# First lot's radial network among the senders' features, all statistics in front, edge indices and three tiles' gram products behind

## The chip, the cores and the metric

The kernel runs on one core of one Trainium2 chip. The metric is the device time of one execution in microseconds (us). Engines: PE is TensorE (matmul), PEld its weight load, DVE is VectorE, ACT is ScalarE, POOL is GpSimd, SP is SyncE; DMAs are issued by SP, ACT and POOL. A "q" behind an engine's name (SPq, ACTq) means its instruction queue, where DMA issues stand.

## The reference, cut to what matters

A network of two layers over 1250 nodes with 512 features. Each layer adds a graph part and a linear attention to the layer-normed features, then a layer of experts. The change lies in the first graph part, which has 41250 edges:

```python
xn = _layernorm(x, axis=-1)
x0, x1 = _lin_irreps(x0, x1, W_up0, W_up1)          # of xn: the senders' features
h = edge_feats                                       # 8 per edge
for W in (W_mlp1, W_mlp2, W_mlp3):                   # the radial network
    h = SILU_2MOM * jax.nn.silu(h @ W / jnp.sqrt(jnp.float32(W.shape[0])))
tpw = h @ W_mlp4 / jnp.sqrt(jnp.float32(W_mlp4.shape[0]))
w1, w2, w3, w4 = jnp.split(tpw, 4, axis=-1)
s0 = x0[sender]
s1 = x1[sender]
# p1 to p4: products of w1 to w4, s0, s1 and four edge attributes
msg0 = jax.ops.segment_sum(m0, receiver, num_segments=num_nodes)
msg1 = jax.ops.segment_sum(m1, receiver, num_segments=num_nodes)
```

The attention of this layer has no softmax, so the kernel needs of the nodes only the gram matrix xn^T xn (512 x 512).

## The kernel before

**Nodes.** The nodes stand in ten tiles of 125 rows. `PIECES` groups tiles 0, 1 to 2, 3 to 5 and 6 to 9, as they are loaded. For a piece, `piece` computes the statistics of its tiles (BN_STATS and BN_AGGR on DVE, one Sqrt on ACT, one reciprocal on DVE), and then `sender(t)` for each tile: DVE makes the normed features xn (L296, L297); PE transposes them (ptr, L302); DVE copies the result to xT (L303); PE multiplies it with the up-weights (pu, L306); ACT scales it to us (L309) and issues two DMAs that write it to xup in DRAM; PE adds the tile's share to the gram matrix in four products (L312), whose accumulators pga, pgb and pgf stay in PSUM for all ten tiles.

**Edge indices.** After the third piece, an `issue_after` block holds the index work: w4b's last quarter is scaled (L331), the receivers (dg) are cast and reduced to a smallest and a largest receiver for each group of seven edge tiles, PE brings these to all partitions (pg, L343), and DVE derives base, rel, idx, the source's quarter (shi, slo) and code from them (L345 to L389, `window`).

**The edge loop.** 323 edge tiles of 128 edges go through `edges`, two at a time; 16 tiles are a lot, with one run of the radial network for it. `layer(b, l, h)` is layer l of lot b: PE into two "net" banks of PSUM, then two Silus on ACT (half of h each, from a buffer of four). For a tile, `product` gathers the senders' rows from xup (POOL, sg, L443) and multiplies h with w4b (pw, L448); `messages` forms msg on DVE (L454 and L457); `gather` multiplies msg with masks sy into pd (L591 to L597); every seven tiles pd is added to agg in DRAM by an indirect DMA (L602). The masks of a group come from `factors` (oh, sy; DVE and ACT, L428 to L436). Six sg buffers let POOL run ahead. Layers of the next lot are issued at tiles 0, 4 and 8 of a lot, the edge features (ef) of the lot after that at tile 6; at tile 10 of each lot but the first, one of `steps` is issued (loads, then the attention's small products). Lot 0's network stands in front of the loop, behind the last piece (L416 to L419), and then four copies of the gram matrix to gs (L420).

**Order and queues.** The tile framework's scheduler places each instruction on its engine's queue, in the program's order as far as its own costs and the `issue_after` marks allow. An engine's queue is strictly in order. SP issues the loads, the clearing of agg (13 DMAs, 6.6 MB) behind the edge features of lots 0 and 1, later loads for the steps, and the clearing of adj behind the edge features of lot 3. The eight semaphores of the hardware DMA queues are shared by SP's and ACT's DMAs, one outstanding DMA each: an issue waits until the DMA before it on its semaphore has landed, whichever engine issued that one. PSUM has two "mm" banks (pga and pgb, later pd), two "net" banks (pu, pg, ph) and four "in" banks (pgf; ptr, later pw).

Of the kernel before, what the change touches and what calls it, by code (L numbers as in the profile page):

```python
# [10 lines left out]
F32 = mybir.dt.float32  # L11
# [3 lines left out]
AF = mybir.ActivationFunctionType  # L15
OP = mybir.AluOpType
# [6 lines left out]
P = 128  # L23
R = 125
NT = N // R
# [4 lines left out]
EG = -(-ET // GT)  # L30
BT = 2 * GT
HID = 64
# [24 lines left out]
def tile_graph_layers(ctx: ExitStack, tc: tile.TileContext, i: dict, out: bass.AP):  # L57
# [17 lines left out]
    def ps_tile(tag, name):  # L75
        return ps_[0].tile([P, 512], F32, tag=tag, bufs=ps_[1][tag], name=name)
# [131 lines left out]
    with ExitStack() as s0:  # L208
# [82 lines left out]
        def sender(t):  # L291


            xn = ew.tile([P, D], F32, tag="xn", bufs=3, name="xn")
            q = dict(scalar1=mvs[:R, t, 0:1], scalar2=rss[:R, t:t + 1], op0=OP.subtract, op1=OP.mult)
            V.tensor_scalar(xn[:R, :P], X[:R, t, :P], **q)  # L296
            last[0] = V.tensor_scalar(xn[:R, P:].rearrange("p (m u) -> p m u", m=3),  # L297
                                      X[:R, t, P:].rearrange("p (u m) -> p m u", m=3), **q)
            ps = in_tile("ptr")
            v = ps[:, :4 * R].rearrange("p (k r) -> p k r", k=4)  # L300
            for k in range(4):
                T.transpose(v[:, k, :], xn[:R, k * P:(k + 1) * P], ident[:R, :R])  # L302
            V.tensor_copy(xT[:, :, t * R:(t + 1) * R], v)  # L303
            pu = ps_tile("net", "pu")
            for k in range(4):
                T.matmul(pu[:R, k * P:(k + 1) * P], xT[:, k, t * R:(t + 1) * R], wu[:, min(k, 1), :],  # L306
                         start=True, stop=True)
            us = ew.tile([P, D], F32, tag="us", bufs=4, name="us")
            S.mul(us[:R], pu[:R], 1.0 / math.sqrt(P))  # L309
            spread(nc.scalar, xup.rearrange("(p t) d -> p t d", t=NT)[:, t, :], us[:R])  # L310
            for pg, a, b, k in gram:
                T.matmul(pg[:, a:b], xn[:R, k * P:(k + 1) * P], xn[:R, k * P:], start=t == 0 and a == 0,  # L312
                         stop=t == NT - 1, skip_group_check=True)

        last = [None]

        def piece(a, b):
            with tc.issue_after(last[0].ins) if last[0] else ExitStack():
                for t in range(a, b):
                    st = ew.tile([P, V.BN_STATS_DIM], F32, tag="bst", bufs=3, name="n0s")  # L320
                    V.bn_stats(st[:R], X[:R, t, :])
                    V.bn_aggr(mvs[:R, t, :], st[:R])
                S.activation(rss[:R, a:b], mvs[:R, a:b, 1], AF.Sqrt, bias=eps[:R], scale=1.0)
                V.reciprocal(rss[:R, a:b], rss[:R, a:b])
            for t in range(a, b):
                sender(t)

        for a, b in PIECES[:3]:
            piece(a, b)
        with tc.issue_after(last[0].ins):  # L330
            V.tensor_scalar(w4b[:, 3 * P:], w4b[:, 3 * P:], 1.0 / math.sqrt(3.0), None, op0=OP.mult)  # L331

            dgf = ew.tile([NG, GW * P], F32, tag="h", bufs=4, name="dgf")
            V.tensor_copy(dgf, dg)
            ext = ec.tile([NG, 2], F32, name="ext")
            V.tensor_reduce(ext[:, 0:1], dgf, AX.X, OP.min)
            V.tensor_reduce(ext[:, 1:2], dgf, AX.X, OP.max)
            V.tensor_tensor(ext[:, 1:2], ext[:, 1:2], ext[:, 0:1], op=OP.subtract)
            extb = ec.tile([NG, 2, P], F32, name="extb")
            V.tensor_copy(extb, ext[:, :, None].to_broadcast([NG, 2, P]))  # L340
            pg0 = ps_tile("net", "pg0")
            for a in range(2):
                T.matmul(pg0[:, a * NG:(a + 1) * NG], extb[:, a, :], ident[:NG, :NG], start=True, stop=True)  # L343
            base = ec.tile([P, 2, NG], F32, name="base")
            V.tensor_copy(base, pg0[:, :2 * NG].rearrange("p (a g) -> p a g", a=2))  # L345
            npf = ec.tile([P, 1], F32, name="npf")
            V.tensor_reduce(npf, base[:, 1, :], AX.X, OP.max)
            npi = ec.tile([P, 2], I32, name="npi")
            V.tensor_copy(npi[:, 0:1], npf)
            V.tensor_scalar(npi[:, 1:2], npi[:, 0:1], 5, None, op0=OP.arith_shift_right)  # L350
            V.tensor_scalar(npi[:, 0:1], npi[:, 1:2], 1, None, op0=OP.add)


            pc = ec.tile([P, 3], I32, name="pc")
            G.iota(pc[:, 0:1], pattern=[[0, 1]], base=0, channel_multiplier=1)
            V.tensor_scalar(pc[:, 1:2], pc[:, 0:1], 5, None, op0=OP.arith_shift_right)
            V.tensor_scalar(pc[:, 2:3], pc[:, 0:1], W - 1, None, op0=OP.bitwise_and)
            pcf = ec.tile([P, 3], F32, name="pcf")
            V.tensor_copy(pcf, pc)
            rows = ec.tile([P, 1], F32, name="rows")  # L360
            V.scalar_tensor_tensor(rows, pcf[:, 1:2], float(NPAD), pcf[:, 2:3], op0=OP.mult, op1=OP.add)


            EP = NG * GW
            rel = ec.tile([P, EP], F32, name="rel")
            V.memset(rel, 0.0)
            V.tensor_copy(rel[:, :ET], dstc)
            rel3 = rel.rearrange("p (g j) -> p g j", j=GW)
            V.tensor_tensor(rel3, rel3, base[:, 0, :, None].to_broadcast([P, NG, GW]), op=OP.subtract)
            srcf = ec.tile([P, ET], F32, name="srcf")  # L370
            V.tensor_copy(srcf, srcc)
            shi = ec.tile([P, ET], F32, name="shi")
            V.tensor_scalar(shi, srcf, float(LO), None, op0=OP.is_ge)
            for c in (2, 3):
                V.scalar_tensor_tensor(shi, srcf, float(c * LO), shi, op0=OP.is_ge, op1=OP.add)
            V.scalar_tensor_tensor(slo[:, 0, :], shi, -float(LO), srcf, op0=OP.mult, op1=OP.add)
            V.scalar_tensor_tensor(slo[:, 1, :], shi, float(LO), srcf, op0=OP.mult, op1=OP.subtract)
            bs = ec.tile([P, NG], F32, name="bs")
            cd = ec.tile([P, 2, ET], F32, name="cd")

            def window(code, idx):

                V.tensor_scalar(bs, base[:, 0, :], float(N), rows, op0=OP.min, op1=OP.add)
                V.tensor_copy(idx, bs)
                V.tensor_scalar(cd[:, 0, :], rel[:, :ET], 0.0, None, op0=OP.is_ge)
                V.scalar_tensor_tensor(cd[:, 0, :], rel[:, :ET], float(W), cd[:, 0, :], op0=OP.is_lt, op1=OP.mult)
                V.scalar_tensor_tensor(cd[:, 1, :], shi, float(W), rel[:, :ET], op0=OP.mult, op1=OP.add)
                V.scalar_tensor_tensor(cd[:, 1, :], cd[:, 1, :], 1.0, cd[:, 0, :], op0=OP.add, op1=OP.mult)
                V.tensor_scalar(code[:, :ET], cd[:, 1, :], -1.0, None, op0=OP.add)  # L389

            def layer(b, l, h):

                two = range(min(2, EG - 2 * b))
                ps = [ps_tile("net", "ph") for _ in (two if l != 1 else range(2))]
                half = [slice(0, HID), slice(HID, P)]
                if l == 0:
                    for q in two:
                        r = slice(32 * q, 32 * q + 16)  # L400
                        T.matmul(ps[q], w1b[r], h[r].rearrange("k j e -> k (j e)"), start=True, stop=True)
                else:
                    w = (w2b, w3b)[l - 1]
                    for q in two:
                        for p in range(2):

                            a, c = (q, p) if l == 1 else (p, q)
                            T.matmul(ps[c][half[a]], w[half[c]], h[half[c], a, :], start=True, stop=True)  # L408
                o = ew.tile([P, 2, 512], F32, tag="h", bufs=4, name="h")
                for n, x in enumerate(ps):  # L410
                    r = slice(0, HID * len(two)) if l == 1 else slice(0, P)
                    S.activation(o[r, n, :], x[r], AF.Silu, scale=1.0 / math.sqrt(8.0) if l == 0 else SILU_2MOM / 8.0)  # L412
                return o
            window(code0, idx0)
        piece(*PIECES[3])
        first = efs[0][0]  # L416
        with tc.issue_after(last[0].ins):
            for l in range(3):
                first = layer(0, l, first)  # L419
        for pg, a, b, k in gram:  # L420
            S.copy(gs[:, k, k * P:], pg[:, a:b])

# [1174 lines left out]
```

## Time and profile before

| | us |
|---|---|
| median of 3 runs (lowest to highest) | 2175.81 (2175.56 to 2176.47) |
| the profiled execution's own time | 2173.73 |
| its span, first to last instruction | 2171.9 |
| first sender product (pu) on PE | 13.6 |
| last write of xup issued | 54.5 |
| first gather of senders' rows (sg) | 58.2 |
| first message (L454) | 67.4 |
| first product of messages (pd) | 69.0 |
| last message of the edge loop | 588.7 |
| mean granted clock of TensorE | 0.973 |

The profile is of one execution; its times are us from its first instruction. A line of the timeline has the start, the duration, engine, source line, operation, output and inputs, the number of instructions merged, and in brackets the idle time before and what ended it. A line of the table by stages has the stretch, its length and then the busy time of each engine with the number of its instructions.

### The profile page before, as it was taken

Reading aid. Unit: us, or ns where it says so; the run is one execution under the profiler, and the core shown is the slowest. Engines: PE = TensorE matmul, PEld = TensorE weight load, DVE = VectorE, ACT = ScalarE, POOL = GpSimd, SP = SyncE. Lnnn points to the kernel's source line nnn. Section 1 sums busy time; section 2 is a strip of 40 time slices with the busy share of each in tenths; the row PEclk is TensorE's granted clock in tenths of the full one; section 3 lists DMA queues with packets and bytes.
Section 4 is the critical chain, followed back from the end, with each engine's and each line's share of the span. In section 5 each row is a group of like instructions: output and inputs, shape, how many; then the busy total and the mean of one; then the engine's idle time right before and its main releaser. Section 6 shows DMA issues by size and latency. Waiting matters only on the chain. (4 is left out here: it accounts for less than half of the span.)

```text
span 2171.9 us, 29920 instructions
## 1 busy us (share of the span) xinstructions
PE 2039.8 (94%) x11341; PEld 1109.4 (51%) x11341; DVE 891.1 (41%) x1864; ACT 640.7 (29%) x1665; POOL 635.3 (29%) x589
## 2 busy tenths in 40 slices
PE   7899999989886899999998999978999999999999
PEld 5334444434364646565566666644446655444354
DVE  7688888868757323232233300004000124670000
ACT  3443444434222424243343311115112121241000
POOL 1677777787600323222322211102000020002000
PEclk9899999989997899999999999989999999999999
DMA  8977777757653875958376312413001040200000
GB/s 257 309 203 179 203 200 189 191 137 189 156 146 104 268 225 153 280 145 239 70 235 165 71 25 64 141 31 111 1 0 64 15 95 0 65 7 1 14 14 19
DMA packets 132866, 270.60 MB, mean 125 GB/s; under 512 B 22028, under 2 KB 45396, under 8 KB 132569
## 3 DMA queue, kind: packets, MB, share of 16 engines
q0 software_dynamic: 48048, 124.53, 24.3%
q1 hardware_dynamic: 82952, 140.78, 20.3%
q10 hardware_dynamic: 1694, 3.07, 0.5%
q8 instruction: 99, 1.62, 0.3%
q14 instruction: 73, 0.60, 0.1%
HBM read 248.73 MB, written 44.76 MB: 135 GB/s over the span
## 5 line engine op out<-in xcount | busy, mean ns | idle before, releaser
L443 POOL DMA_INDIRECT sg<-xup,srcc x323 | 311.7, 965 | 165.9 <-issue 63.0
L457 DVE TENSOR_TENSOR msg<-pw,sg 128x768 f32<-128x768 f32 x323 | 305.4, 946 | 0.0
L971 PE MATMUL phd<-hu,ew 128*128 128x256 f32 x1280 | 292.9, 385 | 10.3 <-ACT hd L972 8.0
L979 PE MATMUL pye<-ew,hd 128*128 128x512 f32 x640 | 287.3, 593 | 0.0
L971 PEld LDWEIGHTS phd<-hu,ew 128*128 128x128 f32 x1280 | 243.8, 193 | 50.1 <-ACT hd L972 14.6
L591 PE MATMUL pd<-msg,sy 128*32 128x320 f32 x646 | 215.9, 448 | 29.3 <-DVE msg L457 28.5
L593 PE MATMUL pd<-msg,sy 128*32 128x256 f32 x1938 | 197.8, 394 | 0.0
L448 PE MATMUL pw<-w4b,h 64*128 64x512 f32 x646 | 187.0, 655 | 0.0
L979 PEld LDWEIGHTS pye<-ew,hd 128*128 128x128 f32 x640 | 117.5, 190 | 124.3 <-issue 122.8
L454 DVE TENSOR_TENSOR msg<-pw,sg 128x256 f32<-128x256 f32 x323 | 134.5, 416 | 78.0 <-PE pw L448 38.8
L436 ACT ACTIVATE sy<-oh,y 128x32 f32<-128x32 f32 x646 | 145.9, 312 | 6.1 <-DVE oh L428 3.3
L204 POOL DMA_INDIRECT adj<-sa,idx x47 | 81.6, 1736 | 220.4 <-ACT sa L203 122.9
L200 DVE TENSOR_SCALAR los<-iol,slo 128x314 f16<-128x314 f16 x230 | 58.2, 304 | 199.4 <-PE pa L201 199.4
L591 PEld LDWEIGHTS pd<-msg,sy 128*32 128x32 f32 x646 | 54.4, 109 | 161.5 <-DVE msg L457 93.6
L972 ACT ACTIVATE hd<-phd,b 128x256 f32<-128x256 f32 x160 | 75.8, 474 | 174.5 <-PE phd L971 174.5
L1414 PE MATMUL pyf<-w,hd 128*125 128x512 f32 (+1 forms) x280 | 125.1, 599 | 0.0
L991 POOL DMA_INDIRECT xrow<-yo,slot x23 | 36.3, 1577 | 298.6 <-ACT yo L990 284.9
L1400 PE MATMUL ph<-uT,w 128*128 128x500 f32 (+3 forms) x336 | 120.8, 515 | 1.1 <-ACT hd L1402 1.0
L989 DVE TENSOR_TENSOR yo<-pye,b 128x512 f32<-128x512 f32 x20 | 13.8, 690 | 244.4 <-PE pye L979 231.3
L597 PEld LDWEIGHTS pd<-msg,sy 128*32 128x32 f32 x1938 | 80.7, 112 | 56.0 <-issue 4.0
L412 ACT ACTIVATE h<-ph 128x512 f32<-128x512 f32 (+1 forms) x124 | 68.2, 591 | 135.5 <-PE ph L408 93.7
L597 PE MATMUL pd<-msg,sy 128*32 128x64 f32 x1938 | 94.1, 221 | 0.0
(424 smaller groups left out, 2650.1 us busy)
## 6 DMA issues: line engine op xcount, KB each, us to landing
ew<-in_L_ffn_W SPq DMA_DIRECT2D x104, 1024.0 KB
agg<-zero SPq DMA_DIRECT2D x12, 512.0 KB
adj<-zero SPq DMA_DIRECT2D x12, 512.0 KB
ag<-agg SPq DMA_DIRECT2D x10, 560.0 KB
ad<-adj POOLq DMA_DIRECT2D x10, 547.8 KB
sg<-xup,srcc POOLq DMA_INDIRECT x323
g<-in_L_gnn_W SPq DMA_DIRECT2D x4, 1024.0 KB
w<-in_L_ffn_W SPq DMA_DIRECT2D x4, 852.5 KB
```

The costliest lines, as they stand in the source:

```text
L436: S.mul(sy[:, j, c, :], oh[:, j, :], y4[:, t0 + j, c:c + 1])
L443: G.indirect_dma_start(out=sg, out_offset=None, in_=xup[:, :], in_offset=bass.IndirectOffsetOnAxis(ap=srcc[:, t:t + 1], axis=0))
L448: T.matmul(pw, h[hb:hb + HID, q, (j // 2) * P:(j // 2 + 1) * P], w4b[hb:hb + HID, :], start=True, stop=True)
L454: V.tensor_tensor(msg[:, :, 0, :], w_[:, 0], sg[:, None, :P].to_broadcast([P, 2, P]), op=OP.mult)
L457: V.tensor_tensor(msg[:, :, 1:, :], w_[:, 1, :, None, :].to_broadcast(q), s1[:, None].to_broadcast(q), op=OP.mult)
L591: T.matmul(d[:W, :SW], sy[:, j, 0, :], mf.rearrange("p a u -> p (a u)")[:, :SW], **q)
L593: T.matmul(d[c * W:(c + 1) * W, :2 * P], sy[:, j, c, :], mf[:, 4:5 + c:c, :], start=j == 0, stop=False, skip_group_check=True)
L597: T.matmul(d[c * W:(c + 1) * W, 2 * P:SW], sy[:, j, 0, :], mf.rearrange("p a u -> p (a u)")[:, a:a + 64], start=False, stop=q["stop"], ski ...
L971: mm = T.matmul(ph[:, :UT], ew1[q][:, k, f * P:(f + 1) * P], hu[:, k, :], start=k == 0, stop=k == 3)
L979: mm = T.matmul(py, hd[q][:, f, a * P:(a + 1) * P], ew2[q][:, f, :], start=q == 0 and f == 0, stop=q == 3 and f == 3)
L1400: mm = T.matmul(ph[:m, :c], w1[k][:, f * P:f * P + m], uT[:, k, c0:c1], start=k == 0, stop=k == 3)
L1414: T.matmul(py[:R], hd[f][:m, r0:r0 + R], w2[f // 4][:m, f % 4, :], start=f == 0, stop=f == FT - 1)
```

## The change

`piece` is split into `stats` (the statistics) and the loop over the tiles. The statistics of the last piece are now issued with those of the third, in front of tiles 3 to 5. `sender` returns its gram products as a function; they are called at once for tiles 0 to 6, and for tiles 7 to 9 after all senders. `layer` is moved up unchanged, and lot 0's three layers, with the scaling of w4b, are issued after tile 5. The index work now stands behind all senders and their gram products.

```diff
             spread(nc.scalar, xup.rearrange("(p t) d -> p t d", t=NT)[:, t, :], us[:R])
-            for pg, a, b, k in gram:
-                T.matmul(pg[:, a:b], xn[:R, k * P:(k + 1) * P], xn[:R, k * P:], start=t == 0 and a == 0,
-                         stop=t == NT - 1, skip_group_check=True)
+
+            def grams():
+                for pg, a, b, k in gram:
+                    T.matmul(pg[:, a:b], xn[:R, k * P:(k + 1) * P], xn[:R, k * P:], start=t == 0 and a == 0,
+                             stop=t == NT - 1, skip_group_check=True)
+            return grams
 
         last = [None]
 
-        def piece(a, b):
+        def stats(a, b):
             with tc.issue_after(last[0].ins) if last[0] else ExitStack():
                 for t in range(a, b):
...
                 V.reciprocal(rss[:R, a:b], rss[:R, a:b])
+
+        def layer(b, l, h):
...
+            return o
+        later = []
+        for n, (a, b) in enumerate(PIECES):
+            if n < 3:
+                stats(a, b)
+            if n == 2:
+                stats(*PIECES[3])
             for t in range(a, b):
-                sender(t)
-
-        for a, b in PIECES[:3]:
-            piece(a, b)
+                later.append(sender(t))
+
+                if t < NT - 3:
+                    later.pop()()
+                if t == 5:
+                    first = efs[0][0]
+                    with tc.issue_after(last[0].ins):
+                        V.tensor_scalar(w4b[:, 3 * P:], w4b[:, 3 * P:], 1.0 / math.sqrt(3.0), None, op0=OP.mult)
+                        for l in range(3):
+                            first = layer(0, l, first)
+        for x in later:
+            x()
         with tc.issue_after(last[0].ins):
-            V.tensor_scalar(w4b[:, 3 * P:], w4b[:, 3 * P:], 1.0 / math.sqrt(3.0), None, op0=OP.mult)
 
             dgf = ew.tile([NG, GW * P], F32, tag="h", bufs=4, name="dgf")
...
-            def layer(b, l, h):
...
             window(code0, idx0)
-        piece(*PIECES[3])
-        first = efs[0][0]
-        with tc.issue_after(last[0].ins):
-            for l in range(3):
-                first = layer(0, l, first)
         for pg, a, b, k in gram:
             S.copy(gs[:, k, k * P:], pg[:, a:b])
```

The order of instructions on each engine, before and after, differs only in the first part of the program, up to the first two lots of the edge loop. There, PE has lot 0's layer 0 behind tile 5, its layers 1 and 2 among tile 6's products, then the transposes of tiles 7 to 9, one gram product, the three tiles' pu, the other gram products, pg, layer 0 of lot 1 and the first pw. DVE has the casts and reductions of dg in front of the xT copies of tiles 7 to 9, and the four sums ssum (L500) among the index work; of the masks, two groups stand in front of the first messages, where there were three with the oh of three more. On SP, the edge features of lots 2 and 3 stand in front of most loads for the steps, and the clearing of adj behind those loads.

## Prediction

> **What bounds the kernel now.** The page says that PE works 94% of the span, and its chain of waits only reaches the last expert layer, so what the change is worth must be read at the start.
>
> ```profile
> span 2171.9 us, 29920 instructions
> PE 2039.8 (94%) x11341; PEld 1109.4 (51%) x11341; DVE 891.1 (41%) x1864; ACT 640.7 (29%) x1665; POOL 635.3 (29%) x589
> ```
>
> Next, the busy time by stages (columns: PE, PEld, DVE, ACT, POOL, then granted clock, DMA share, GB/s):
>
> ```profile
> 32.00:36.40 4.40, 0.92 (x6) 0.52 (x4) 4.40 (x20) 1.29 (x6) 0.00 (x0) 1.00 1.03 389
> 36.40:42.00 5.60, 4.99 (x19) 3.45 (x20) 5.60 (x13) 3.76 (x18) 0.00 (x0) 0.70 1.01 376
> 42.00:53.30 11.30, 11.30 (x63) 7.67 (x61) 6.09 (x9) 6.90 (x24) 0.00 (x0) 1.00 0.88 289
> 53.30:65.30 12.00, 8.32 (x27) 2.28 (x26) 4.70 (x7) 6.60 (x15) 5.54 (x6) 0.68 0.89 242
> 65.30:73.40 8.10, 8.10 (x53) 2.88 (x54) 4.87 (x8) 1.60 (x4) 3.84 (x5) 0.63 0.66 229
> 73.40:95.00 21.60, 17.53 (x231) 7.84 (x232) 16.37 (x28) 8.95 (x35) 14.59 (x15) 1.00 1.03 398
> 95.00:120.00 25.00, 23.32 (x294) 10.19 (x291) 23.46 (x41) 9.98 (x37) 17.92 (x18) 1.00 0.82 227
> 120.00:300.00 180.00, 173.97 (x2003) 78.38 (x1998) 154.75 (x268) 77.15 (x285) 134.73 (x128) 0.99 0.74 193
> ```
>
> The edge loop runs at PE's pace once it is under way (97% from 120 to 300 us); before it PE waits twice, at 33 to 36 and from 53 to 65, and pays with a low clock each time. The timeline names the waits:
>
> ```profile
> 32.27 0.64 PE L343 MATMUL pg<-ident,extb 47*128 47x47 f32 x4
> 36.41 0.33 PE L302 MATMUL ptr<-ident,xn 125*128 125x125 f32 x1 [3.50 <-DVE xn L296]
> 58.24 1.06 POOL L443 DMA_INDIRECT sg<-xup,srcc  x1 [50.12 <-DMA w<-in_L_mix_Wk]
> 65.28 3.79 PE L448 MATMUL pw<-w4b,h 64*128 64x512 f32 x8
> 67.39 0.42 DVE L454 TENSOR_TENSOR msg<-pw,sg 128x256 f32<-128x256 f32 x1 [8.08 <-PE pw L448]
> ```
>
> Tile 6's features wait for DVE's index work. Later the radial network, a chain PE to ACT to PE from 53.33, holds the first pw until 65.28 and the first message until 67.39, while the gathers have been coming since 58.24. The loop then meets the clearing of adj:
>
> ```profile
> 81.60:95.10 13.50, 5.87 (x7) 1.00 1.03 393
> 95.10:118.10 23.00, 15.12 (x16) 1.00 0.81 236
> DMA packets 2762, 9.43 MB, mean 377 GB/s; under 512 B 374, under 2 KB 502, under 8 KB 2761
> q1 hardware_dynamic: 1666, 6.11, 61.7%
> q0 software_dynamic: 1095, 3.31, 37.6%
> ```
>
> The first two lines are the long half of the messages (L457): 1.93 us a tile at a DMA share of 1.03, then 1.44 us. The others are all transfers of 70 to 95 us: SP's clears take 0.244 MB/us of 0.377.
>
> **The change, part by part.** No instruction is added or dropped, and from about 130 us on every engine's order is the old one; the sum is how much earlier the loop runs.
>
> *All statistics in front.* Four BN_STATS at 0.60 us start to start, four aggregations and a reciprocal, some 2.9 us, move ahead of tile 3's features. DVE waited 0.28 and 1.95 us for grams there, so most is covered: following DVE's order, tile 3's xT copy ends about 0.8 us later, and PE with it. Without that cover 2.9. Tile 5's grams end at 32.3 + 0.8 = 33.1.
>
> *The index work leaves.* PE no longer waits 3.50 us before tile 6, and 36.4 to 42 is not run at 0.70.
>
> *The network comes in.* Layer 0 costs PE 1.13 (row at 53.33) and is done at 34.2; tile 6's transposes and two grams fill PE until 36.4. ACT copies tile 5 (0.60), issues two xup writes (0.31 and up to 1.26, as at 32.70), loads its table (1.28) and runs Silu, 0.55 a half: the first half is there at 36.7. Layer 1 (1.09) ends at 37.8, the rest of tile 6's grams at 38.6, layer 2 at 39.9; tile 6's pu waits for a "net" bank and ends at 41.1. Behind ACT's Silus waits tile 6's copy, whose write goes out near 41.8, as before (42.32). What leaves is the chain of 12 us at 53.3.
>
> *Tiles 7 to 9.* Transposes 3 x 0.59, one gram 0.9, three pu at 1.1: 47.1. The xT copies stand behind index casts and two reductions on DVE: tile 9's features need tile 6's grams (38.6), 0.95 + 3.3 us of index work, and three copies at 0.6: 44.8, in time. The last xup write is issued at 49.2 to 50.5 instead of 54.51; write to first gather took 3.4 us (54.82 to 58.24), so the gathers start at about 53.3, 5 us earlier. Their flight no row shows alone; it lies between nothing and the 9.2 us from 58.24 to the first message. I take 4, in the lower half, since less else is in flight there than at 81.60 to 95.10: 57.3. On SP the edge features of lots 2 and 3 move ahead of lnb and Wk; lot 3's wait for lot 1's layer 0 (about 55), and the loads of wo, Wk, bk and bl and the clears of adj queue behind them until about 60 to 64.
>
> *Grams and indices behind.* The grams left, 1.4 + 2.3 + 2.3 (a tile's four rows at 28 to 32 us), end at 53.1, pg at 53.6. DVE has meanwhile done the source indices and ssum (4 x 1.39) by 52.7, so base waits for PE. Then, start to start from the rows of 32.95 to 36.51: base to the second cd 2.2, sb 0.4, oh 0.28, cd, sy, code and oh 1.5: the first message half begins at 58.0 instead of 67.39. One sy stands between its halves: L457 at 58.9 instead of 67.73. ACT's fourteen sy (3.08) run from 56.5 to 59.6. First pd at 59.9 instead of 68.99: **9 us earlier**.
>
> *Given back in lots 0 and 1.* DVE gets four oh, one sy, kvb and bqb, 2.5 us that lay in idle time. Where DVE sets the pace (95 to 120: 23.46 of 25) that costs up to 2.5, where gathers do, nothing; I take 0.5, since gathers do until 95. Those loads, 1.8 MB, ran in front of the loop and now fall into it. At 0.244 MB/us that is 7.4 us more of SP traffic, which also starts some 8 us earlier (62 instead of 70), so it ends near 95 again. Tiles by then: five at 62, then 33 / 1.93 = 17, so tile 22 where now it is tile 16, of which I count 5.5 ahead: 5.5 x 1.44 = 7.9, less 0.5, gives **7.5**. Bounds: 3.6 if the 1.8 MB cost the gathers their full time at 377 GB/s (4.8) and DVE its 0.5 on top of a 9 us gain, and 12 if the old clock of 0.63 (8.1 us, so 3.0 lost) goes as well and nothing is given back.
>
> The Trainium skill speaks against this part ("DMA: Bandwidth & Descriptors", Rules for kernel authors): transfers issued from different engines run on the same 16 DMA engines and interleave. By that rule the earlier gathers only share what is there and the sum would be nearer 2172; the row of 81.60 to 95.10 agrees that they share.
>
> Span 2171.9 - 7.5 = 2164.4; the profiled execution had 1.83 around its span, so 2166.2; the median of the runs lies 2.08 above that execution: **2168.3**.
>
> **Rivals.** *The transfers take it:* the loop starts 9 us earlier, but gathers, loads and clears move the same bytes at 377 GB/s, so only some 3.6 us are kept: 2172.2. For: share 1.03 and three DVE waits on sg between 80 and 95. Against: by the DMA shares over time the engines are half idle at 47 to 49 and 68 to 72 us, and the change fills these gaps.
>
> *More than forecast:* PE keeps its clock and the clears don't slow the first lots: 11 us, 2164.8. Against: the waits on sg.
>
> *A cold PE at the start of the loop:* after the first pw PE stands about 2.2 us before the first pd. If base comes 1.3 us later than I have it, this becomes the 3.5 us after which the clock was 0.70 for 5.6 us: 1.7 + 1.3 lost, 2171.3. The Trainium skill ("TensorE: Matmul & The Clock Gate", the HAM clock gate) puts the limit at one idle window of about 3.4 us; the 3.50 us row agrees.
>
> *Slower:* tiles 7 to 9's xup writes share semaphores with clears of agg, and each waits until an earlier one landed. In the old run tile 5's second issue took 1.26 us amid the clears. If the clears still fill the queue at 46 to 50, the writes queue behind one another, each up to 5.9 us (SP's own longest wait on such a write); three in a row put the gathers at 64 instead of 53.3 and, with 4 us of flight, messages at 68, and the loads inside the loop then cost 4.8: 2181. It decides from gathers later than 58 on. Against: 12 x 0.5 MB at 380 GB/s from 28 us are through by 47.
>
> **How the numbers follow.** Forecast 0.61, transfers 0.17, more 0.08, cold PE 0.06, slower 0.08. About 0.2% (4.35 us) is what a measurement of this kernel can tell from no change; that is below 2171.5 and above 2180.2. Of the forecast nine tenths lie below 2171.5, and all of "more", half of "cold" and a quarter of "transfers": 0.55 + 0.08 + 0.03 + 0.04, about 0.70. Slower 0.07; the rest 0.23. The range leaves out the end of "more" (0.07) and "slower" with the tail of "transfers" (0.12): 2163.0 to 2174.5.
>
> **What would show it.** Right: no 3.5 us idle of PE before tile 6's transposes; first gather near 53, first L454 near 58 with base released by pg, first pd near 60; L457 of tile 16 near 86 and of tile 22 near 95; the loop's last message 7 to 8 us before 588.7; later stages of equal length. Wrong: gathers after 58, a PE clock under 0.8 at the start of the loop, or the lead of 9 us at tile 0 shrunk under 4 by tile 32.

## The result, and the profile after

| | before | after |
|---|---|---|
| median of 22 runs, us (lowest to highest) | 2176.41 (2171.12 to 2180.08) | 2173.21 (2169.56 to 2176.10) |
| ratio, 95% interval | | 0.9986 (0.9980 to 0.9993) |
| the profiled execution's own time, its span | 2173.73, 2171.9 | 2176.02, 2174.2 |

The change gains 3.1 us (1.5 to 4.4 by the interval): inside the range, the right sign, and less than half of the 7.5 forecast; it is under the 0.2% that was to count as faster. The profiled execution of the changed kernel happens to be one of its longest, that of the kernel before one of its shorter ones, so the spans are not compared; the stretches are.

The same stretches of the changed kernel (columns PE, PEld, DVE, ACT, POOL, granted clock, DMA share, GB/s):

```profile
32.00:36.40 4.40, 4.40 (x24) 2.62 (x23) 1.72 (x3) 1.78 (x2) 0.00 (x0) 1.00 1.01 362
36.40:42.00 5.60, 4.57 (x25) 1.63 (x24) 2.35 (x9) 3.26 (x7) 0.00 (x0) 1.00 1.02 391
42.00:53.30 11.30, 11.30 (x69) 8.61 (x67) 11.30 (x18) 3.40 (x8) 0.00 (x0) 1.00 0.86 305
53.30:65.30 12.00, 9.15 (x44) 3.18 (x48) 8.61 (x25) 8.71 (x35) 8.51 (x7) 0.88 0.60 158
65.30:73.40 8.10, 7.93 (x62) 2.95 (x58) 4.66 (x9) 0.00 (x0) 3.99 (x6) 0.54 1.01 405
73.40:95.00 21.60, 17.21 (x221) 7.31 (x217) 18.57 (x35) 11.78 (x48) 14.90 (x15) 1.00 1.04 402
```

The first stall is gone: PE is busy for all of 32 to 36.4, and 36.4 to 42 runs at full clock where it was 0.70. Behind it the DMA engines, not PE, have changed most: from 53.3 to 65.3 they are busy for 0.60 (0.89 before), and from then on they are full, 1.01 in a stretch where the kernel before had 0.66. The timeline has the steps:

```profile
34.65 0.65 PE L302 MATMUL ptr<-ident,xn 125*128 125x125 f32 x4
53.88 0.26 DVE L385 COPY base<-pg 128x94 f32<-128x94 f32 x1 [0.33 <-PE pg L383]
54.97 1.06 POOL L455 DMA_INDIRECT sg<-xup,srcc  x1 [46.86 <-DMA ef<-in_edge_attr]
59.20 0.42 DVE L466 TENSOR_TENSOR msg<-pw,sg 128x256 f32<-128x256 f32 x1 [0.92 <-DMA sg<-xup,srcc]
61.08 0.46 PE L603 MATMUL pd<-msg,sy 128*32 128x320 f32 x1 [2.85 <-DVE msg L469]
70.85 2.07 PE L460 MATMUL pw<-w4b,h 64*128 64x512 f32 x4
```

Tile 6's transposes no longer wait 3.50 us; base is released by pg; the first message half starts at 59.20 (67.39 before) and now waits for its gather, not for pw. The first pd is 7.9 us earlier (61.08, was 68.99). PE stood 2.85 us in front of it, and the last line shows what follows: at a granted clock of 0.50 the four instructions of two tiles' pw take 2.07 us, where they take 1.13 at full clock (at 75.09 in the same trace). The long half of the messages, L469 now, by stretches:

```profile
81.60:95.10 13.50, 6.64 (x7) 1.00 1.04 395
95.10:118.10 23.00, 16.10 (x17) 1.00 0.87 246
```

All transfers of 70 to 95 us (packets, MB and share by queue; q1 carries SP's, q0 the gathers):

```profile
DMA packets 3114, 10.09 MB, mean 404 GB/s; under 512 B 461, under 2 KB 635, under 8 KB 3111
q1 hardware_dynamic: 1760, 5.97, 59.7%
q0 software_dynamic: 1351, 4.07, 43.3%
```

From 81.6 to 95.1 a tile takes 1.93 us, as before, and the clears of adj that were to be over near 95 have two pieces issued at 98.33. So the lead of the start does not last. In the next table each row is the start of the messages' long half (us), with the lead over the kernel before; the first four runs of the experiments stand under it.

| | tile 0 | 3 | 8 | 14 | 20 | 28 | 64 | 128 |
|---|---|---|---|---|---|---|---|---|
| before | 67.7 | 71.3 | 79.4 | 90.2 | 101.9 | 112.5 | 172.6 | 273.1 |
| after | 60.1 (7.6) | 68.6 (2.7) | 77.6 (1.8) | 86.1 (4.1) | 97.9 (3.9) | 108.9 (3.6) | 169.3 (3.4) | 269.9 (3.2) |
| e1, network only | 62.5 (5.3) | 70.7 (0.6) | 83.1 (-3.8) | 91.5 (-1.3) | 101.4 (0.5) | 112.5 (0.1) | 172.4 (0.2) | 272.9 (0.2) |
| e2, index work only | 62.0 (5.7) | 65.6 (5.7) | 74.3 (5.1) | 83.0 (7.2) | 94.5 (7.3) | 107.0 (5.5) | 167.8 (4.9) | 268.2 (4.9) |
| e3, warm PE | 60.7 (7.0) | 65.6 (5.7) | 77.1 (2.3) | 85.3 (4.9) | 98.6 (3.2) | 109.9 (2.6) | 169.8 (2.8) | 270.2 (2.8) |
| e4, clears later | 59.6 (8.2) | 64.9 (6.5) | 76.7 (2.7) | 84.7 (5.6) | 93.6 (8.2) | 105.0 (7.5) | 163.9 (8.8) | 267.6 (5.4) |

The 3.2 to 3.4 us of the changed kernel at tiles 64 and 128 fit the 3.1 us measured. Behind tile 128 the table stops: from there to the loop's last message these six profiles took 314.0 to 317.9 us for the same work, and the changed kernel's lead at the last message was 0.9. Single executions scatter that much; e12, below, is a second profile of the changed kernel.

### The profile page after: what moved, and what is told of

The parts are those of the page before. It is cut to its first block, busy times and chain, and to the rows that moved or that the text cites. A ratio compares the mean times of both kernels' runs of the same rounds, so it can differ in the third digit from the quotient of the medians.

```text
span 2174.2 us, 29922 instructions
## 1 busy us (share of the span) xinstructions
PE 2041.1 (94%) x11341; PEld 1109.1 (51%) x11341; DVE 891.1 (41%) x1864; ACT 640.7 (29%) x1665; POOL 636.1 (29%) x589
## 5 line engine op out<-in xcount | busy, mean ns | idle before, releaser
L455 POOL DMA_INDIRECT sg<-xup,srcc x323 | 313.2, 970 | 163.3 <-issue 64.3
L469 DVE TENSOR_TENSOR msg<-pw,sg 128x768 f32<-128x768 f32 x323 | 306.6, 949 | 0.0
L983 PE MATMUL phd<-hu,ew 128*128 128x256 f32 x1280 | 292.8, 385 | 11.2 <-ACT hd L984 9.0
L204 POOL DMA_INDIRECT adj<-sa,idx x47 | 81.6, 1736 | 214.5 <-ACT sa L203 123.9
L1001 DVE TENSOR_TENSOR yo<-pye,b 128x512 f32<-128x512 f32 x20 | 13.8, 690 | 244.4 <-PE pye L991 231.3
```

What stands on the lines that cost most here:

```text
L455: G.indirect_dma_start(out=sg, out_offset=None, in_=xup[:, :], in_offset=bass.IndirectOffsetOnAxis(ap=srcc[:, t:t + 1], axis=0))
L469: V.tensor_tensor(msg[:, :, 1:, :], w_[:, 1, :, None, :].to_broadcast(q), s1[:, None].to_broadcast(q), op=OP.mult)
L983: mm = T.matmul(ph[:, :UT], ew1[q][:, k, f * P:(f + 1) * P], hu[:, k, :], start=k == 0, stop=k == 3)
```

## Experiments: where the lead goes

Two theories. *Cold PE*: the lead is lost because PE's clock falls at the start of the loop. *Transfers*: it is lost because gathers, loads and clears share the DMA engines, which are full from 65 to about 100 us. e1 to e4 ran together on one chip, beside the kernel before (median 2176.66). The kernel before took 2176.41 in the runs of the result, so both are called the first chip here, though it is not known that they are the same.

**e1: the network alone.** The kernel before, with `layer` moved up and

```diff
         for a, b in PIECES[:3]:
             piece(a, b)
+        first = efs[0][0]
         with tc.issue_after(last[0].ins):
             V.tensor_scalar(w4b[:, 3 * P:], w4b[:, 3 * P:], 1.0 / math.sqrt(3.0), None, op0=OP.mult)
+            for l in range(3):
+                first = layer(0, l, first)
...
         piece(*PIECES[3])
-        first = efs[0][0]
-        with tc.issue_after(last[0].ins):
-            for l in range(3):
-                first = layer(0, l, first)
```

> The kernel before, with only the first lot's radial network moved behind tile 5's features; statistics, index work and grams are issued where they were. Both theories on where the lead goes (a cold PE at the start of the loop; transfers) agree on the first message: the chain of 12 us at 53.3 is gone, so the gathers bound it, and as the xup writes stay where they were (first gather 58.24 before, flight 4.2 us as in the changed kernel) it starts at 62.5, 5 us before the old 67.39. If the lead shrinks by the same 4.5 us as in the changed kernel, next to nothing is left: 2176, ratio 1.00. If the moved index work is needed for nothing, it equals the changed kernel: 2173.2, ratio 0.9986. I expect 2175, ratio 0.9993.

Measured: 2176.22, ratio 0.9999 (0.9986 to 1.0012). The first message came as expected (62.11; the long half at 62.5), and 0.5 us of the lead was left at tile 20. PE's clock fell between 58 and 59 us, behind a wait of 1.78 us; PE then waited 3.82 us for the first pd, and the clock stayed at 0.50 until about 82:

```profile
65.30:73.40 8.10, 7.58 (x34) 2.15 (x32) 5.48 (x10) 0.00 (x0) 3.96 (x6) 0.50 1.02 410
73.40:95.00 21.60, 20.65 (x203) 8.32 (x202) 14.56 (x26) 7.66 (x29) 12.20 (x12) 0.80 1.02 390
```

Here PE is busy at half clock, and the DMA engines are full as well, so this run alone does not tell the theories apart. It does show that taking the network's 12 us off the path leaves 0.2 us at tile 64 by itself; the interval of the times does not rule out 3 us.

**e2: statistics, grams and index work alone.** The changed kernel, with

```diff
-                if t == 5:
-                    first = efs[0][0]
...
             window(code0, idx0)
+            V.tensor_scalar(w4b[:, 3 * P:], w4b[:, 3 * P:], 1.0 / math.sqrt(3.0), None, op0=OP.mult)
+        first = efs[0][0]
+        with tc.issue_after(last[0].ins):
+            for l in range(3):
+                first = layer(0, l, first)
```

> The changed kernel without the moved network: statistics in front, three tiles' grams and the index work behind, and the network after them, before the loop. The stall of 3.5 us before tile 6 leaves, so the grams end near 50 and the network's chain of 12 us runs from 50 to 62: first pw at 62, first message half at 64, lead 3.4 us at tile 0, PE cold at the start as in the kernel before. Cold PE: the cold stretch is the same as before, so the lead is kept: 2173.2, ratio 0.9985. Transfers: gathers are there long before, and the clears start as early as in the changed kernel: the lead shrinks to 2, 2174.5. If the moved index work brings nothing by itself: 2176.4.

Measured: 2172.82, ratio 0.9983 (0.9973 to 0.9993): as good as the whole change. The long half of tile 0 is 2 us later than with the whole change, but the first gather is out at 50.78 and the next ones follow from 55.87, under the network's chain, so the first four messages come 1.2 us apart. And it keeps its lead (4.9 at tile 64) although PE's clock is low for as long as in the kernel before, only earlier: 0.57 from 53.3 to 65.3, and 1.00 from there to 73.4, where the changed kernel has 0.54:

```profile
53.30:65.30 12.00, 11.05 (x52) 3.81 (x56) 8.03 (x15) 9.86 (x40) 8.80 (x8) 0.57 0.72 198
```

The DMA engines stand idle for 3.4 of these 12 us, against 4.8 in the changed kernel: SP issues bc, wo and wr ahead of lot 3's edge features here, and behind them there. By its expectation a lead that is kept (5.7 at tile 0, 4.9 at tile 64) spoke for the cold PE, and one that shrinks to 2 for transfers; the interval of the time holds both. So this run is a point against transfers as they were put there. The 1.4 us less of idle DMA time had not been counted, and no run on this chip moves those loads alone.

**e3: a warm PE.** The changed kernel, with

```diff
+WARM = 5
...
                 sy, d = mask[g], now["d"]
+                if first and t == 0:
+                    for _ in range(WARM):
+                        T.matmul(d, h[0][:, 0, :P], h[0][:, 0, :], start=True, stop=True, skip_group_check=True)
```

> The changed kernel with five matmuls of 64... no: 128 x 512 more on PE behind the first four pw, into the bank of the first pd, which overwrites them: 2.8 us of work in the 2.85 us in which PE stood idle ahead of the first pd. Cold PE: the clock stays over 0.95 from 62 to 73, where it was 0.54 to 0.65; tile 3 and those behind it no longer wait 2.53 us for pw, the lead at L469 of tile 8 is 5 us or more where it was 1.8, and the run takes 2169.5 to 2170.5, ratio 0.997. Transfers: the clock is full, but the messages wait for sg in place of pw, the lead at tile 20 is 4 as in the changed kernel, and the time is its 2173.2, ratio 0.9986.

Measured: 2173.39, ratio 0.9987 (0.9975 to 0.9999), the changed kernel's. The five matmuls took 4.56 us (56.87 to 61.43) and kept the clock up; by stretches:

```profile
53.30:65.30 12.00, 11.27 (x65) 4.54 (x64) 8.75 (x25) 7.42 (x32) 8.65 (x7) 1.00 0.67 171
65.30:73.40 8.10, 4.80 (x68) 2.19 (x68) 7.11 (x15) 4.03 (x16) 5.25 (x6) 0.95 0.96 368
73.40:95.00 21.60, 18.00 (x197) 7.32 (x199) 15.67 (x28) 8.86 (x34) 14.22 (x15) 0.90 1.03 403
```

What DVE waited for between 58 and 100 us (total us, times, longest), here and, in the last two lines, in the changed kernel:

```profile
DVE msg L467 <- DMA sg<-xup,srcc: 7.9, 5, 4.0
DVE msg L467 <- PE pw L461: 3.0, 2, 1.8
DVE msg L466 <- DMA sg<-xup,srcc: 7.0, 7, 2.6
DVE msg L466 <- PE pw L460: 2.8, 2, 2.5
```

The clock is 0.95 where it was 0.54, tile 3 comes 3 us earlier, and by tile 8 all but 0.5 us of that is gone: PE has little work (4.80 of 8.10), and the longest wait of the messages, 4.0 us, is for a gather. The clock then falls for some 4 us all the same (0.90 from 73.4 to 95, where the changed kernel has 1.00), so the low clock is not gone but halved: from 53.3 to 95 us it costs 2.6 us of full clock here, 5.1 in the changed kernel. With that much taken away, the time is unchanged; a cold PE alone does not explain the lost lead.

**e4: the clears later.** The changed kernel, with each piece of adj's clearing behind the edge features of lot 5 to 17:

```diff
-                nc.sync.dma_start(v[:, a:b], zero[:, :b - a])
+                with tc.issue_after(behind[a // 1024][1].ins) if behind else ExitStack():
+                    nc.sync.dma_start(v[:, a:b], zero[:, :b - a])
...
-            clear(adj.rearrange("a b -> (a b)"), 4 * NPAD * LO)
+            clear(adj.rearrange("a b -> (a b)"), 4 * NPAD * LO, [efs[5 + n] for n in range(13)])
```

> The changed kernel with the 13 pieces of the clearing of adj issued one by one, each behind the edge features of a later lot (5 to 17), in place of all together from 63.66 us on. Transfers: between 73 and 95 us the DMA share falls from 1.03 to about 0.6, the long half of the message comes every 1.44 us where it was 1.9, which for 11 tiles is 5 us; 2168, ratio 0.9963. Cold PE: the clock is still 0.5 to 0.65 from 62 to 73 and the lead at tile 8 is 2 us as in the changed kernel; what is gained after that is under 1.5 us: 2172, ratio 0.998.

Measured: 2173.32, ratio 0.9986 (0.9973 to 0.9998). In the trace transfers are right: tile 20 has the whole 8.2 us of lead, and tile 28 comes at 105.0. The clock did not do as expected, though; it is full from 65.3 us on:

```profile
65.30:73.40 8.10, 5.68 (x84) 2.53 (x73) 4.38 (x8) 0.00 (x0) 4.03 (x5) 1.00 1.01 405
73.40:95.00 21.60, 19.89 (x248) 8.54 (x240) 20.92 (x39) 12.90 (x50) 15.44 (x15) 1.00 0.69 177
```

So this run has both, a warmer PE and no clears, and it is to be read against e3, whose PE was warm from 53 to 72 us with the clears in place. Up to tile 8 the two and the changed kernel have lost alike (leads of 2.3, 2.7 and 1.8), with the loads of Wk, wo, bk and bl in the way in all three. From tile 8 to tile 20 e4 wins 5.5 us over the kernel before, e3 0.9, and the gathers show why: between tiles 16 and 24 they take 5.3 us from issue to message here, 8.9 in e3 and 8.2 in the changed kernel. Whether the clears' absence would do as much with a cold PE, no run on this chip shows.

From 66 us to tile 28, in the kernel before:

```profile
66.00:112.50 46.50, 40.75 (x478) 17.23 (x478) 37.20 (x63) 15.40 (x55) 30.17 (x29) 0.94 0.90 312
```

In the changed kernel:

```profile
66.00:108.90 42.90, 38.14 (x442) 15.83 (x436) 36.11 (x64) 17.30 (x67) 28.68 (x28) 0.92 1.00 364
```

And in this one:

```profile
66.00:105.00 39.00, 34.38 (x432) 14.78 (x434) 34.41 (x63) 17.38 (x67) 26.91 (x26) 1.00 0.76 223
```

With the clears in place the changed kernel's DMA engines are full in all of this stretch; at the 364 GB/s that they reached, its bytes need all of it. The bytes are the same in each kernel: from 14 us to the long half of tile 28 the kernel before moved 28.18 MB, the changed one 28.24, e1 28.07, e2 28.17 and e3 28.11; e4 moved 21.44. In the kernel before and in the changed one:

```profile
14.00:112.50 98.50, 84.97 (x693) 44.87 (x695) 73.17 (x149) 38.20 (x122) 36.00 (x35) 0.91 0.86 286
14.00:108.90 94.90, 86.26 (x696) 45.01 (x698) 73.54 (x149) 37.91 (x122) 37.58 (x35) 0.95 0.86 298
```

Length less length times share gives the idle time of the DMA engines, to about 0.5 us: 13.3 us in the changed kernel, 15.8 in e1, 11.2 in e2 and 14.4 in e3 (shares 0.84, 0.88 and 0.85), and tile 28 follows it: 108.9, 112.5, 107.0 and 109.9. The kernel before does not fit in. It idles 13.8 us, 0.5 more than the changed kernel, but its bytes take 84.7 us of busy time where the other four take 81.5 to 82.7. So most of the 3.6 us of lead at tile 28 is the same bytes moved faster (346 GB/s of busy time, 333 before), not idle time filled; what made them faster, no run shows.

The time of e4, though, is no better than the changed kernel's. Some of the lead goes when the pieces come (8.0 at tile 96, 5.4 at tile 128); the rest lies within an interval that is 5 us wide, and stays open. That the clears cost the change its lead is thus shown for the trace up to tile 64, not for the time.

**On two other chips.** The later runs fell on a second chip (e5 to e11; the kernel before took 2288.81 us) and a third (e12 to e15; 2300.28). What is slower there is the edge loop alone. e5 is the kernel before, unchanged:

> The kernel before, unchanged, for a second profile of it. In its first one the loop from tile 64 to its end took 416.1 us, and from the loop's end to the span's end 1583.2; the five other kernels so far, the same code from there on, took 414.4 to 418.5 and 1585.2 to 1587.3. If those differences are scatter of single executions, this profile lies among the others in the second figure (1585 to 1587). If the older front really makes later stages shorter, it is 1583 again. Up to tile 28 the first message halves should repeat within 1 us (long half of tile 28 at 112.5).

Behind the loop it took 1584.8 us, between the 1583.2 of the first profile and the 1585.2 to 1587.3 of the others: the differences look like scatter. The loop from tile 64 on took 518.8 us in place of 416.1. From 130 to 300 us in the first profile of the kernel before:

```profile
130.00:300.00 170.00, 164.28 (x1884) 74.37 (x1876) 146.24 (x254) 71.58 (x266) 126.89 (x120) 0.99 0.74 192
```

The same stretch in e5:

```profile
130.00:300.00 170.00, 156.56 (x1504) 65.33 (x1506) 118.53 (x200) 59.15 (x216) 101.47 (x98) 0.94 0.61 161
```

What POOL's gathers waited for there (a message that gives its sg buffer back; 14.7 us in the first profile):

```profile
POOL sg L443 <- DVE msg L457: 44.0, 33, 3.2
```

From a gather's issue to its message go 9.5 us here (tiles 64 to 128), 6.1 in the first profile. There are six sg buffers, a message takes 1.28, and the next gather into its buffer is issued 1.15 later: (9.50 + 1.28 + 1.15) / 6 = 1.99 us a tile, measured 1.98. Such a sum comes out for any loop over six buffers (in the first profile (6.1 + 1.28 + 2.2) / 6 = 1.6, measured 1.57), since the flight holds all that a message waits for; it shows where a tile's time is spent, and not by itself what sets the pace. That it is the gathers here rests on their longer flight and on 44.0 us of waiting for a buffer; but only 33 of 86 gathers waited so, and PE is still busy for 92% of this stretch. So the gathers' flight over six buffers probably sets the loop's pace on these chips from about tile 16 on, and what frees DMA time shows less; no run with more buffers tells. The remaining runs, by the start of the long half (us):

| | chip | tile 0 | 14 | 28 | 64 | median | ratio (95%) |
|---|---|---|---|---|---|---|---|
| e5, before | second | 67.9 | 92.2 | 119.1 | 190.2 | | |
| e6, warm and clears later | second | 59.7 | 85.3 | 113.3 | 185.2 | 2286.22 | 0.9985 (0.9973 to 0.9997) |
| e8, loads early | second | 63.5 | 88.5 | 117.7 | 187.4 | 2287.03 | 0.9999 (0.9984 to 1.0014) |
| e11, four clears first | second | 61.9 | 88.7 | 117.8 | 189.5 | 2286.81 | 0.9990 (0.9978 to 1.0002) |
| e12, after again | third | 59.4 | 85.9 | 114.6 | 187.5 | 2297.24 | 0.9987 (0.9974 to 0.9999) |
| e13, clears behind the loop | third | 59.2 | 85.6 | 113.3 | 187.0 | 2311.44 | 1.0041 (1.0026 to 1.0056) |
| e14, the same and warm | third | 59.8 | 85.6 | 114.6 | 185.9 | 2312.82 | 1.0052 (1.0033 to 1.0071) |
| e15, before, clears behind | third | 67.5 | 90.4 | 119.7 | 192.7 | 2316.36 | 1.0061 (1.0043 to 1.0078) |

**e6: both edits.** The diffs of e3 and e4 together.

> The changed kernel with both edits at once: five matmuls ahead of the first pd, and the pieces of adj's clearing each behind the edge features of a later lot. If transfers alone bound the first lots, PE's clock has no say and this equals the run with the clears alone: long half of tile 20 at 93.6, tile 28 at 105.0, 2173.3. If with the clears gone the cold PE is the next limit, tile 20 is at 90 to 91 and tile 28 at 102, some 3 us earlier, and the time 2170.5, ratio 0.9973. Warmth alone had brought nothing to tile 28 (109.9 against 108.9).

No 3 us more: tile 20 at 100.2, and the ratio is that of the changed kernel. On this chip that decides little: tiles 14 to 20 came 2.5 us apart with the clock at 1.00 and a DMA share of 0.68 (81.6 to 95 us), so something other than either theory, most likely the gathers' flight (7.7 us, where e4 had 5.5), held them.

**e8 and e11: fill the DMA engines' gap.** The changed kernel with `loads()` called in front of `edges(True, idx0)` in place of the first step (e8), or with

```diff
             clear(agg.rearrange("a b -> (a b)"), 4 * NPAD * SW)
+            clear(adj.rearrange("a b -> (a b)"), 4 * NPAD * LO, 0, 4096)
...
-            clear(adj.rearrange("a b -> (a b)"), 4 * NPAD * LO)
+            clear(adj.rearrange("a b -> (a b)"), 4 * NPAD * LO, 4096)
```

where the last two arguments bound the pieces (e11).

> The changed kernel with the loads of lnb, bc, wo, wr, br, Wk, bk and bl (2.3 MB) issued on SP's queue ahead of the edge features of lots 2 and 3, so that they no longer wait behind lot 3's. In five kernels 28.1 to 28.2 MB had been moved by the long half of tile 28, and the time of it followed the idle share of the DMA engines; in the changed kernel they idle 5 us of 53 to 66. Transfers: 1.8 MB go into that gap, at 377 GB/s 4.8 us, less what they delay the xup writes and first gathers: the DMA share of 53 to 66 rises from 0.61 to 0.85 or more, tile 28 comes at 105.5 where it was at 108.9, and the time is 2170, ratio 0.997. Cold PE: the clock stays low for 10 us after the first gathers and tile 28 comes at 108 or later, 2173.

> The changed kernel with four of the 13 pieces of adj's clearing (2.1 MB) issued right behind agg's, so from about 47 us on in place of 63.7. Transfers: the DMA engines' idle time of 42 to 66 is filled (share 0.85 or more from 53 to 66), and though the xup writes and the first gathers share with them and the first message comes some 2 us later (61 to 62), tile 28 comes at 105 to 106 where it was at 108.9; 2170, ratio 0.997. If the start of the loop decides: the first message 2 us later and a PE that idles longer put tile 28 at 110 or later and the time at 2175.

Both missed. The gap was filled (DMA share 0.88 in 53 to 66 with e8; with e11 0.97 in 42 to 53, and 0.71 in 53 to 66), but the first gather went out at 55.83 and 57.20 (54.02 in e12), the long half of tile 0 came at 63.5 and 61.9 (59.4), and tile 28 was later than in e12 by 3 us, though on another chip of about the same pace. What goes ahead of the last xup writes and first gathers seems to hold them up by as much as it saves.

**e12: the changed kernel again.**

> The changed kernel, unchanged, for a second profile and time of it. Its first profile had a lead of 7.6 us at tile 0, 3.6 at tile 28, 3.4 at tile 64 and 0.9 at the loop's end, and stages behind the loop 3 us longer than the kernel before, while the times of both kernels say 3.1 us. If the losses behind tile 64 are scatter of single executions, the lead at tile 28 repeats within 1 us on a chip like the first one, the later ones don't, and the ratio is 0.9986 again. If something in the change costs time there, the lead shrinks from tile 64 on again.

The ratio repeats, 0.9987, on a chip with a slower loop. The lead at single tiles cannot be repeated there, as the kernel before was not profiled on that chip; against e15, which is the kernel before without the clears in the loop, tile 28 is 5.1 us ahead. From tile 128 to the last message it took 390.9 us, the unchanged kernel before 391.8 on the second chip, so nothing here says that the change costs time late in the loop.

**e13 to e15: the clears behind the loop.** Pieces of adj's clearing in `route`, from tile 3 on, for the changed kernel (e13), for it with e3's matmuls (e14) and for the kernel before (e15):

```diff
-            clear(adj.rearrange("a b -> (a b)"), 4 * NPAD * LO)
...
             spread(nc.sync, xrow[t * R:(t + 1) * R, :], X[:R, t, :])
+            if t > 2:
...
+                for a in range((2 * t - 6) * 1024, min((2 * t - 4) * 1024, f), 1024):
...
+                    nc.sync.dma_start(v[:, a:b], zeros[:, :b - a])
```

> The changed kernel with the 13 pieces of adj's clearing taken out of the loop, to the routing steps behind it, where the DMA share is 0.3 to 0.6. (For an order of edges that needs a second window, which this input's does not, the counts of that window would be wiped out; for this input nothing is left out.) Transfers: the first lots no longer wait, tile 28 comes at 104 to 105 where it was at 108.9, nothing is given back in the loop, and the lead of 7.5 us lasts: 2169, ratio 0.9966. If the start of the loop decides (cold PE, gathers), tile 28 is at 108 and the time 2172.5.

> The same with five matmuls ahead of the first pd, so that PE's clock stays full. If PE's clock is the next limit once the clears are gone, tiles 3 to 8 come 3 us earlier than in the run without them, tile 28 at 102, and the time is 2166.5, ratio 0.9955. If the loads of Wk, bk, bl and wo and the gathers still bound the start, tile 28 is at 104 to 105 as without them, and the time is the same, 2169.

> The kernel before with the clearing of adj behind the loop in the same way, which tells what the change is worth when the clears are out of the way. The first message stays at 67.5. Transfers: the 22 us of clearing from 70 to 95 no longer hold the gathers, tile 28 comes at 108 to 109 where it was at 112.5, 2172.5, ratio 0.9983; the changed kernel is then still 4 us ahead (104 to 105), a little more than the 3.1 measured with the clears in the loop. If the clears cost the kernel before nothing, since its lots start late, it stays at 112.5 and 2176, and the change is worth 7.5.

All three missed. In the loop the clears' absence brought 1.3 us at tile 28 to the changed kernel and nothing to the one before (119.7 against the 119.1 of e5, on another chip). Flights say why: between tiles 16 and 24 the changed kernel's gathers take 9.4 us with the clears and 9.3 without, where on the first chip it was 8.2 and 5.3 (e4). And behind the loop the clears stand on SP's queue ahead of the next tile's rows of agg: routing took 77.4, 79.7 and 77.9 us in e13 to e15 from its first tile to its last, and 64.0 in e12 (64.0 to 64.3 in the kernel before, the changed kernel, e4, e5, e6, e8 and e11, on all three chips). Of these 13 us the profile names 5.2 as a wait of PE between 735 and 850 us, which e12 does not have:

```profile
PE pm L690 <- DMA ag<-agg: 5.2, 2, 3.6
```

No version here beats the changed kernel beyond the intervals; e2, without the moved network, is level with it.

## Why the prediction was right or wrong, point by point

- *All statistics in front* and *the index work leaves*: right. Layer 0 starts at 33.50 behind tile 5's grams (33.1 forecast), and the stall and the clock of 0.70 are gone.
- *The network comes in*: right in kind, 0.9 to 1.7 us short. From their first matmul to their last, its layers took 1.22, 1.57 and 1.48 us on PE where 1.13, 1.09 and 1.09 were taken, and the table load began only at 35.22; tile 6's pu ended at 42.8 (41.1 forecast).
- *Tiles 7 to 9*: that delay, and a second xup issue of 1.64 us at 46.84, put the last write's issue at 51.07 (49.2 to 50.5) and the first gather at 54.97 (53.3).
- *The flight of 4 us*: 4.23, from 54.97 to 59.20. *Base waits for PE*: right, 53.88 behind pg.
- *First message at 58.0, pd at 59.9, 9 us earlier*: 59.20, 61.08 and 7.9.
- *Given back in lots 0 and 1*: here the sum failed, and with it the 7.5 us; that 2173.2 still lies in the range is due to the room that the range leaves for the transfers rival, not to this sum. It forecast tile 22 near 95 us, "5.5 ahead", for 7.5 us kept; the long half that starts at 95.2 is tile 18's, two ahead, and 3.4 us were kept. Two things were mis-sized. "Five at 62" took the first tiles at 1.93 us each; at 62.5 only tile 1 began, and tiles 0 to 4 came 2.7 us apart, for lack of gathers and then of clock. And the clears were given one fixed end near 95, with the gathers' share left as before; the engines were idle for 4.8 us of 53.3 to 65.3, where SP's loads stood behind lot 3's edge features, and full thereafter, so the clears ended later.
- *Rival: the transfers take it.* This comes nearest: 3.6 us kept by its sum (9, less 4.8, less 0.5, is 3.7), 2172.2; measured 3.4 at tile 64 and 2173.2. e4 bears out its mechanism in the trace, but giving the transfers room gained no time. Its counter-argument, that the change fills the gaps at 47 to 49 and 68 to 72 us, was wrong by halves: it filled the second and opened a larger one at 53 to 66. The rule of the Trainium skill named there ("DMA: Bandwidth & Descriptors", Rules for kernel authors: one set of 16 DMA engines for all issuing queues) spoke for 2172, and the trace agrees: gathers take 8.2 us beside SP's clears and 5.3 without them.
- *Rival: a cold PE.* Its condition was wrong: the clock fell after 2.85 us of idle time, not 3.5, and was 0.54 from 65.3 to 73.4. The kernel before could have told: behind this wait of 2.34 us its clock is 0.50 from 58 us on.

```profile
56.79 2.19 PE L408 MATMUL ph<-h,w2b 64*64 64x512 f32 x8 [2.34 <-ACT h L412]
```

Its price does not show in the time: e3 took half of the low clock away and gained nothing. The Trainium skill's limit of about 3.4 us ("TensorE: Matmul & The Clock Gate", the HAM clock gate) did not hold here as a gap in one piece: the clock fell after 2.85, 2.34 and, in e1, 1.78 us.

- *Rivals: more, slower.* Neither. The last xup write was issued by 51.7 and the first gather at 54.97, short of the 58 from which the slower case was to decide.
- What the prediction left out of its cases: that the parts are not additive. The network's 12 us, its largest term, leaves 0.2 us at tile 64 alone (e1), and the rest alone is worth as much as the whole (e2).

## What to carry to other kernels

When a stage's start is moved ahead, count the bytes that must be moved until a fixed tile of it, and the rate at which they went: the lead that lasts is what the change takes from the DMA engines' idle time until then, or wins by moving the same bytes faster, and not what it takes from the compute chain. A stall that is taken away from a stage with two limits (here a cold PE over late gathers) can show in the trace at once and in the time not at all, so take away both before a price is put on one. And look at how long a gather is under way before its message, over how many buffers: with six, 6.1 us went with 1.57 us a tile here, and 9.5 with 1.98.

## What the runs showed of the hardware

- The same program's gathers took 6.1 us from issue to message on one chip and 9.5 on another, with DMA share 0.74 and 0.61 from 130 to 300 us, and its loop 1.57 and 1.98 us a tile: on the first PE was busy for 97% of that stretch, on the second for 92%, with POOL waiting 44.0 us for buffers (14.7 on the first).
- PE's clock fell after 2.85 us of idle time in one piece, and PE had been busy for 5.24 of the 8 us from 53 to 61; in the kernel before it fell after 2.34 us and in e1 after 1.78. In e2 it fell to 0.50 at 50 us although the profile has PE busy for 10.8 of the 11 us from 40 to 51. Once low it could stay low under load: in e1 PE was busy for 15.1 of 15.6 us (66 to 81.6) at a granted clock of 0.50.
- DMA time that looks free is not free to a queue: 6.4 MB of clears in a stretch with DMA shares of 0.25 to 0.54 (735 to 810 us of e12) cost routing 13 us, in three runs alike, where 16 is what they take at 0.4 MB/us. The rows of agg that the next tile needs stood behind them on SP's queue.
